# Splitting the involution's DMA transfers by partitions

## The chip, the cores and the metric

The kernel runs on one core of a Trainium2 chip. The metric is the device time of one execution in microseconds; where there are several executions, their median counts. A core has five engines with instruction streams of their own: TensorE (PE in the profile; PEld is its weight loads), VectorE (DVE), ScalarE (ACT), GpSimd (POOL) and SyncE (SP, which here only issues DMAs). Sixteen DMA engines move the data.

## The reference, cut to what matters

The input x is float32 of 8 x 256 x 56 x 56. Layer 0 adds an involution of the normalised x to x; layer 1 adds a residual block of two ternary 3x3 convolutions with batch norm. Only layer 0 is touched by the change:

```python
x = x + _L0_conv_ref(_gn(x), w_reduce, b_reduce, w_span, b_span)     # involution, 7x7, 16 groups
x = x + _L1_conv_ref(_gn(x), w1, w2, g1, b1, g2, b2)                 # two 3x3 convolutions
...
ker = einsum('bchw,oc->bohw', x, w_reduce) + b_reduce                # 256 -> 64 channels
ker = einsum('bchw,oc->bohw', ker, w_span) + b_span                  # 64 -> 16 groups x 49 taps
out = (ker.reshape(B, G, 1, 49, H, W) * patches(xp)).sum(axis=3)     # each pixel has its own 7x7 kernel
```

## The kernel before, in words

The involution (layer 0) comes first, at about 56 to 1108 us of the profile after some 56 us of loads and preparation. The two convolutions and a last pass follow; they read what the involution has stored to HBM (`x1_d`).

The involution goes image by image (8), and in each image through 4 "quarters" of 64 channels, 32 quarters in all. In a quarter the two halves of the image lie on the two halves of the 128 partitions, and 10 rows of tiles (`ty`, each 3 x 8 pixels by 7) are done one after the other. For each row a tile `q` of neighbourhoods is wanted: 126 positions (9 rows by 14 columns around a tile) on the partitions, 7 x 128 values each, read from `x_nb`, which the host lays out. `load_q` issues one DMA of 128 rows (3584 B each) for it; the two rows past 126 belong to the next row or are padding, and nothing reads them. Five buffers (`NQB`) hold q tiles: the tile for row r + 5 is issued by SyncE (`prefetch`) once row r's matmuls have released its buffer. GpSimd then corrects the rims of the tile (`fill_rim`, L752), three rows ahead of its use; for rows 8 and 9 of a quarter ScalarE fills the lower end (`fill_end`, L765), two rows ahead.

TensorE does two things by turns: `apply_row` (pa, L854: 56 small matmuls of q with the kernel matrix `a`) for the present row, and `generate` (pg, L823) for the matrix of the next quarter, whose PSUM results ScalarE (L827) and VectorE (L831) copy into `a` with the bias. ScalarE (L867), VectorE (L868) and GpSimd (L871) bring a row's result out of PSUM and add it onto the image x in SBUF. `reduce` (pk, L711) and the parameters of the next image's normalisation are done in the third quarter (c = 2), from statistics (L143) that VectorE takes of the next image in rows 4 to 19 of the present one.

The order is written out by hand: for each row, in this order, a store of the last quarter's result (`store_x1`, in rows 2 and 3 of a quarter, 64 partitions of 6272 B), or a load of the next image (`load_x`, in rows 0, 1, 4, 5, 7, 8, 14 and 15 of an image, 128 partitions of 3136 B); then `apply_row`, `prefetch`, statistics, `pick_out`, the rims, the steps of `generate`, and one step of the weights' quantisation (loads of 128 x 576 B, L289, and stores of 768 x 192 B, L318). `pin` keeps this order on each engine. All of these DMAs are issued by SyncE, in order. Each takes one of eight completion semaphores by turns and waits until the DMA that had it before, eight issues back, has landed.

Of the kernel before, what the change touches and what calls it, by code (L numbers as in the profile page):

```python
# [17 lines left out]
P = 128  # L18
B, C, H, W = 8, 256, 56, 56
# [9 lines left out]
CH = P // 2  # L29
NCQ = C // CH  # L30
# [3 lines left out]
NHW = HH * W  # L34

PY, PX = 3, 8
TY, TX = 10, W // PX
# [3 lines left out]
QY, QX = PY + K - 1, PX + K - 1  # L41
NQ = QY * QX
# [5 lines left out]
HQ = TY * PY + K - 1  # L48
# [7 lines left out]
NQB = 5  # L56
PLEAD = 2
RIM_AT = 1

NCB = 4  # L60
NC = NHW // NCB
# [22 lines left out]
def involution_tri_block_kernel(  # L84
# [3 lines left out]
    nc = tc.nc  # L88
# [6 lines left out]
    def scratch(name):  # L95
        return [[dram.tile([P, HW], F32, tag=f"{name}_{b}_{t}", name=f"{name}_{b}_{t}")
                 for t in range(CT)] for b in range(B)]

    x1_d, y1_d, y2_d = scratch("x1d"), scratch("y1d"), scratch("y2d")
# [473 lines left out]
    with ExitStack() as ph1:  # L573
# [22 lines left out]
        work = ph1.enter_context(tc.tile_pool(name="work", bufs=2))  # L596
        apool1 = ph1.enter_context(tc.tile_pool(name="apool1", bufs=1))

        def load_x(b, c, j):

            if j == 0:
                xs[b, c] = xpool.tile([P, NHW], F32, tag="x", name=f"x_{b}_{c}")
            part = slice(j * NHW // 2, (j + 1) * NHW // 2)
            nc.sync.dma_start(xs[b, c][:, part], x[b, c, :, part])

        def gn1_stats(b, c, j):

# [56 lines left out]
        prm, xs = {}, {}  # L664
        for c in range(NCQ):
            for j in range(2):
                load_x(0, c, j)
# [28 lines left out]
        for j in range(2):  # L696
            o = j * nf // 2
# [28 lines left out]
        def load_q(b, c, ty):  # L726

            q = qpool.tile([P, TX, P], F32, tag="q", name=f"q_{b}_{c}_{ty}")
            nc.sync.dma_start(q.rearrange("p k c -> p (k c)"),
                              x_nb[b, c, (HQ - QY - PY * ty) * QX:(HQ - QY - PY * ty) * QX + P, :])  # L730
            return q

        def rim_of(b, c):

            sides = work.tile([P, 2, P], F32, tag="sides", name=f"sides_{b}_{c}")
            tops = work.tile([P, 3, CH], F32, tag="tops", name=f"tops_{b}_{c}")
            rim = prm[b][3][:, c]
            for dst, k0, k1, f1 in ((sides, 0, 2, P), (tops, 2, 5, CH)):
                shape = [NQ, k1 - k0, f1]
                nc.gpsimd.tensor_tensor(dst[:NQ], rims_sb[:NQ, k0:k1].unsqueeze(2).to_broadcast(shape),  # L740
                                        rim[:NQ, :f1].unsqueeze(1).to_broadcast(shape), ALU.mult)
            low = work.tile([P, CH], F32, tag="low", name=f"low_{b}_{c}")
            nc.gpsimd.tensor_copy(low[:NQ], rim[:NQ, CH:])
            around[b, c] = sides, tops, low
# [132 lines left out]
        def prefetch():  # L877
            if queue:
                k = queue.pop(0)
                loads[k] = load_q(*k)  # L880
                bare.append(k)

        def surround(keep=PLEAD):
            for k in filled:
                fill_end(*k)
            filled.clear()
            while len(bare) > keep or bare and not queue:
                filled.append(bare.pop(0))
                fill_rim(*filled[-1])

        def store_x1(b, c, h):
            nc.sync.dma_start(
                x1_d[b][c // 2][c % 2 * CH:(c % 2 + 1) * CH, h * NHW:(h + 1) * NHW],
                xs[b, c][h * CH:(h + 1) * CH])

        gst = {}

# [91 lines left out]
        for m, (b, c) in enumerate(quarters):  # L989
# [6 lines left out]
            for ty in range(TY):  # L996
                r = c * TY + ty

                if last is not None and ty in (2, 3):
                    store_x1(*last, ty - 2)  # L1000
                elif more and r in X_AT:
                    load_x(b + 1, X_AT.index(r) // 2, X_AT.index(r) % 2)
                row = apply_row(b, c, a, ty)
                prefetch()

                if r == PARAMS_AT:
                    norm = params(b + 1) if more else gn2_params(0, b)
                next(norm, None)

                if ty == 1 and last is not None:  # L1010
                    gn2_stats(*last, TY)
                elif ty >= 2:
                    gn2_stats(b, c, ty - 1)
                if more and 4 <= r < 20:
                    gn1_stats(b + 1, (r - 4) // NCB, (r - 4) % NCB)
                pick_out(b, c, ty, *row)
                surround()
                if ty == RIM_AT and m + 1 < len(quarters):
                    rim_of(*quarters[m + 1])
                next(norm, None)  # L1020
                for _ in range(PER_ROW[ty]):
                    next(gen, None)
                if m * TY + ty >= QUANT_AT:
                    next(quant, None)
                pin()
# [6 lines left out]
        for h in range(2):  # L1032
            store_x1(*last, h)
# [46 lines left out]
    with ExitStack() as ph4:  # L1080
# [10 lines left out]
        for j in range(B * CT):  # L1091
            b, t = j // CT, j % CT
            y1f, y2f, x1f = (home(name, j) for name in ("y1", "y2", "x1"))
            n = {B * CT - 2: 2, B * CT - 1: 4}.get(j, 1)
# [95 lines left out]
```

## Time and profile before

| what | value |
|---|---|
| median of 3 runs (lowest, highest) | 2209.84 us (2204.62, 2218.38) |
| the profiled execution: time, span | 2220.68 us, 2218.9 us |
| its mean granted TensorE clock | 0.902 |
| TensorE busy over the span | 1765.9 us (80%), 30192 matmuls |
| VectorE, ScalarE, GpSimd busy | 1726.8, 1425.1, 589.8 us |
| q tiles: DMAs, size, median landing | 320, 448 KB, 4.3 us |
| images: DMAs, size, median landing | 64, 392 KB, 5.2 us |
| results: DMAs, size, median landing | 64, 392 KB, 5.5 us |
| one quarter, mean of c = 0, 1, 2, 3 | 30.2, 29.6, 43.1, 27.9 us |

A page of the profile shows one execution. "Busy" counts instructions, not waits. In the list of waits a line such as "ACT q L765 <- POOL q L752: 12.3, 21, 2.1" says that ScalarE was idle before line 765 until GpSimd's line 752 had written q: 12.3 us in total, 21 times, 2.1 us at the longest. "Issue" as the releaser means that the engine was waiting for nothing that the profile names. In the windows each engine has its busy time in the stretch and its count of instructions; behind them stand the granted TensorE clock, the mean busy share of the sixteen DMA engines, and GB/s. A DMA's landing is counted from its issue. The quarters' lengths are from the first pa matmul of one quarter to that of the next.

### The profile page before, as it was taken

The page shows a single profiled execution, that of the slowest core. Times are in us where ns is not written, and L with a number is a line of the kernel's source. Part 1 is how long each engine was busy: PE and PEld are TensorE (multiplying, and loading weights), DVE is VectorE, ACT ScalarE, POOL GpSimd, SP SyncE. Part 2 cuts the span into 40 slices and gives each one's busy share as a digit, 9 for nine tenths or more (in the row PEclk, how much of TensorE's full clock was granted, in tenths as well). Part 3 has the DMA queues.
Part 4 walks back from the last instruction along what each step waited for, and adds up shares of the span by engine and source line. Part 5 has one row for each costly group of instructions (what it writes and reads, how often), then busy time and mean ns, then how long its engine had stood idle before and what let it go on. Part 6 is the DMA issues. An engine that isn't in the chain of part 4 may idle for free.

```text
span 2218.9 us, 71607 instructions
## 1 busy us (share of the span) xinstructions
PE 1765.9 (80%) x30192; PEld 1622.0 (73%) x30192; DVE 1726.8 (78%) x3257; ACT 1425.1 (64%) x3505; POOL 589.8 (27%) x965
## 2 busy tenths in 40 slices
PE   4888898888889888888699999997999999970000
PEld 3676776777667676677599999997999999970000
DVE  5667869686685867756599999998999999984444
ACT  3767677676767767677457666665566666663334
POOL 1546555464654645555500000000000000000000
PEclk9999899899989999899799999999999999995555
DMA  5558768585765757657643333336233333369999
GB/s 179 177 167 250 206 194 250 156 258 180 245 201 166 256 156 242 188 167 207 215 186 119 119 119 118 119 122 212 106 119 119 118 119 124 135 252 414 429 429 396
DMA packets 156252, 440.11 MB, mean 198 GB/s; under 512 B 63774, under 2 KB 74012, under 8 KB 148508
## 3 DMA queue, kind: packets, MB, share of 16 engines
q1 hardware_dynamic: 150336, 405.50, 53.8%
q10 hardware_dynamic: 5596, 30.03, 3.3%
q8 instruction: 239, 3.92, 0.8%
q14 instruction: 81, 0.66, 0.1%
HBM read 323.28 MB, written 112.20 MB: 196 GB/s over the span
## 4 chain that ended last, share of the span: by engine, by line
PE 71%; DMA 10%; DVE 8%; issue 6%; ACT 4%; POOL 0%; SPq 0%; ACTq 0%; DVEq 0%; POOLq 0%
PE c L516 39%; PE pg L823 16%; PE pa L854 10%; PE pk L711 4%; ACT a L827 3%; DMA x1f<-x1d 2%; PE ks L787 2%; DMA y1f<-y1d 2%; DMA out_y<-x1f 2%; DMA y2f<-y2d 2%; DVE a L831 1%; DVE x1f L1103 1%; PE rim L646 1%; DVE st L143 1%; DVE inv L868 1%
## 5 line engine op out<-in xcount | busy, mean ns | idle before, releaser
L516 PE MATMUL c<-pl,wq 128*128 128x392 f32 x4608 | 856.8, 348 | 14.1 <-ACT pl L386 14.1
L516 PEld LDWEIGHTS c<-pl,wq 128*128 128x128 f32 x4608 | 854.8, 189 | 15.8 <-ACT pl L386 14.5
L827 ACT ACTIVATE a<-pg,bt 126x126 f32<-126x126 f32 (+1 forms) x2048 | 528.8, 457 | 113.7 <-PE pg L823 112.0
L823 PE MATMUL pg<-kr,wl 64*126 64x140 f32 (+1 forms) x6144 | 470.1, 297 | 60.7 <-issue 27.8
L823 PEld LDWEIGHTS pg<-kr,wl 64*126 64x126 f32 x6144 | 409.1, 200 | 88.6 <-issue 29.7
L854 PE MATMUL pa<-a,q 126*32 126x48 f32 x17920 | 292.6, 215 | 104.6 <-issue 86.2
L854 PEld LDWEIGHTS pa<-a,q 126*32 126x32 f32 x17920 | 240.8, 117 | 180.0 <-issue 110.0
L831 DVE TENSOR_TENSOR a<-pg,bt 126x504 f32<-126x504 f32 (+4 forms) x640 | 281.3, 481 | 53.7 <-PE pg L823 52.3
L868 DVE SCALAR_TENSOR_TENSOR inv<-pa,gn1s,inv 128x168 f32<-128x168 f32 x320 | 118.3, 370 | 236.2 <-ACT inv L867 235.4
L871 POOL TENSOR_TENSOR x<-x,inv 128x168 f32<-128x168 f32 x320 | 166.6, 521 | 472.5 <-DVE inv L868 386.1
L386 ACT CAST pl<-r 128x812 fp32r<-128x812 f32 x192 | 162.6, 868 | 144.3 <-DVE r L381 124.8
L366 POOL MEMSET xp<- 128x116 f32 x32 | 6.3, 196 | 824.9 <-DVE a L381 824.9
L752 POOL TENSOR_TENSOR q<-q,sides 126x256 f32<-126x256 f32 (+1 forms) x320 | 224.2, 701 | 2.9 <-DMA q<-in_x_nb 2.9
L387 DVE TENSOR_TENSOR pl<-r,pl 128x812 fp32r<-128x812 f32 x192 | 186.8, 999 | 26.5 <-ACT pl L386 25.4
L451 ACT ACTIVATE dummy<-y,nc 128x1568 f32<-128x1568 f32 (+1 forms) x128 | 200.2, 1564 | 4.8 <-DVE y L536 3.5
L867 ACT ACTIVATE inv<-pa,gn1s 128x168 f32<-128x168 f32 x320 | 134.4, 420 | 99.6 <-PE pa L854 72.5
L143 DVE BATCH_NORM_STATS2 st<-x 128x6 f32<-128x392 f32 x256 | 137.8, 554 | 12.3 <-DMA x<-in_x 9.7
L801 POOL TENSOR_TENSOR x<-x,add 128x504 f32<-128x504 f32 (+1 forms) x128 | 127.2, 1025 | 13.1 <-ACT add L795 13.1
L1050 ACT ACTIVATE xp<-raw,gn 128x392 f32<-128x392 f32 (+1 forms) x124 | 82.5, 721 | 58.8 <-DVE a L381 58.8
L1070 ACT ACTIVATE xp<-raw,bi_bn,sc_bn 128x392 f32<-128x392 f32 (+1 forms) x124 | 82.4, 721 | 58.8 <-DVE a L381 57.1
L1101 DVE SCALAR_TENSOR_TENSOR y1f<-y2f,sc_bn,y1f 128x3136 f32<-128x3136 f32 (+2 forms) x20 | 56.6, 2831 | 64.9 <-DMA y2f<-y2d 54.6
L1103 DVE TENSOR_TENSOR x1f<-x1f,y1f 128x3136 f32<-128x3136 f32 (+2 forms) x20 | 55.3, 2771 | 50.2 <-DMA out_y<-x1f 24.2
(174 smaller groups left out, 1791.7 us busy)
## 6 DMA issues: line engine op xcount, KB each, us to landing
q<-in_x_nb SPq DMA_DIRECT2D x320, 448.0 KB, 4.3
raw<-x1d SPq DMA_DIRECT2D x32, 812.0 KB, 6.3
raw<-y1d SPq DMA_DIRECT2D x32, 812.0 KB, 6.5
x<-in_x SPq DMA_DIRECT2D x64, 392.0 KB, 5.2
x1d<-x SPq DMA_DIRECT2D x64, 392.0 KB, 5.5
y1d<-y SPq DMA_DIRECT2D x30, 784.0 KB, 3.8
y2d<-y SPq DMA_DIRECT2D x30, 784.0 KB, 3.3
y1f<-y1d SPq DMA_DIRECT2D x14, 1568.0 KB, 14.3
```

The costliest lines, as they stand in the source:

```text
L143: nc.vector.bn_stats(st[:, j, :], xt[:, j * NC:(j + 1) * NC])
L386: nc.scalar.copy(hi, r)
L387: nc.vector.tensor_tensor(lo, r, hi.bitcast(F32), ALU.subtract)
L451: nc.scalar.activation(dst, v, f, bias=shift[:, to:to + 1], accum_out=stats[:, to, j, n:n + 1])
L516: nc.tensor.matmul(ps[:, to, :NM], wq[k][:, t, dx, to * P:(to + 1) * P], part[:, t, :, dx:dx + W], start=(c == 0), stop=(c == last))
L752: nc.gpsimd.tensor_tensor(v, v, z, ALU.add)
L823: nc.tensor.matmul(dst, wl[rows, c, gp, o:o + NQ], kr[py][rows, px, :], start=True, stop=True)
L827: nc.scalar.activation(dst[:, g + 1, p0 + j], ps[1][:NQ, j * nt + t0:j * nt + t1], AF.Identity, bias=bt[:, c, g + 1, p0 + j:p0 + j + 1])
L831: nc.vector.tensor_tensor(dst[:, g, p0:p0 + n].rearrange("q p t -> q t p"), ps[0][:NQ, t0 * n:t1 * n].rearrange("q (t p) -> q t p", p=n), ...
L854: nc.tensor.matmul(ps[o:o + 32, k * 2 * n:(k + 1) * 2 * n], q[:NQ, k, o:o + 32], av[:, t + k, g * 2 * n:(g + 1) * 2 * n], start=True, stop ...
L868: nc.vector.scalar_tensor_tensor(iv, odd, scale[:, 1:2], iv, ALU.mult, ALU.add)
L871: nc.gpsimd.tensor_tensor(xv, xv, iv.rearrange("p t (y x) -> p y t x", x=PX), ALU.add)
```

## The change

A new helper, `spread`, issues one DMA for each group of partitions, all from SyncE. The q tiles are loaded with 126 partitions instead of 128, in two DMAs whose sizes go by the quarter: 63 + 63 for c = 0, 99 + 27 for c = 1, 108 + 18 for c = 2, 117 + 9 for c = 3. An image's loads become 63 + 63 + 2, a result's stores 63 + 1. The host no longer pads `x_nb`. The instructions of the other engines and their order are the same.

```diff
+SPLITS = ((63, 63), (99, 27), (108, 18), (117, 9))
...
+        def spread(dst, src, cuts):
+
+            p0 = 0
+            for n in cuts:
+                nc.sync.dma_start(dst[p0:p0 + n], src[p0:p0 + n])
+                p0 += n
+
         def load_x(b, c, j):
...
-            nc.sync.dma_start(xs[b, c][:, part], x[b, c, :, part])
+            spread(xs[b, c][:, part], x[b, c, :, part], (63, 63, 2))
...
             q = qpool.tile([P, TX, P], F32, tag="q", name=f"q_{b}_{c}_{ty}")
-            nc.sync.dma_start(q.rearrange("p k c -> p (k c)"),
-                              x_nb[b, c, (HQ - QY - PY * ty) * QX:(HQ - QY - PY * ty) * QX + P, :])
+            o = (HQ - QY - PY * ty) * QX
+            spread(q.rearrange("p k c -> p (k c)"), x_nb[b, c, o:o + NQ, :], SPLITS[(b * NCQ + c) % len(SPLITS)])
             return q
...
         def store_x1(b, c, h):
-            nc.sync.dma_start(
-                x1_d[b][c // 2][c % 2 * CH:(c % 2 + 1) * CH, h * NHW:(h + 1) * NHW],
-                xs[b, c][h * CH:(h + 1) * CH])
+            spread(x1_d[b][c // 2][c % 2 * CH:(c % 2 + 1) * CH, h * NHW:(h + 1) * NHW],
+                   xs[b, c][h * CH:(h + 1) * CH], (63, 1))
...
-    near_rows = np.zeros((B, NCQ, HQ * QX + P - NQ, TX * P), np.float32)
-    near_rows[:, :, :HQ * QX] = near[:, :, ::-1, ::-1].reshape(B, NCQ, HQ * QX, TX * P)
+    near_rows = np.ascontiguousarray(near[:, :, ::-1, ::-1]).reshape(B, NCQ, HQ * QX, TX * P)
```

## The prediction, made before the changed kernel was run

> **What bounds the kernel now.** I read the page's busy table first, then the windows of the involution, then the waits, then the DMA issues, and last the trace's packet records (start, duration, size and queue of each DMA packet; no record names its DMA engine).
>
> The change touches the involution alone, some 56 to 1108 us, and the loads before it. Three stretches (the whole, and one of quarters 0 and 1), with engine busy times, clock, DMA share and GB/s:
>
> ```profile
> 56.00:1108.00 1052.00, 881.26 (x25347) 744.12 (x25343) 746.71 (x2064) 747.06 (x2649) 575.30 (x918) 0.92 0.67 204
> ```
>
> ```profile
> 310.00:390.00 80.00, 66.07 (x2128) 55.02 (x2127) 66.82 (x184) 59.65 (x213) 47.98 (x77) 0.98 0.80 243
> ```
>
> TensorE is busy 84% of the stage, VectorE and ScalarE 71%. The sixteen DMA engines are busy 67%, and 80% where the next image is also loaded. What is late when TensorE idles, over the whole span:
>
> ```profile
> PEld pa L854 <- issue: 110.0, 118, 3.9
> PE pa L854 <- issue: 86.2, 64, 3.7
> ...
> PEld pg L823 <- issue: 29.7, 25, 3.4
> PE pg L823 <- issue: 27.8, 23, 3.2
> ...
> ACT q L765 <- POOL q L752: 12.3, 21, 2.1
> ...
> PEld pa L854 <- POOL q L752: 10.1, 10, 1.6
> ```
>
> "Issue" means that no semaphore was late. (PE and PEld count the same idle time twice.) The reader should see that no DMA of data stands here. What is late is code. Queue 8 carries it:
>
> ```profile
> q8 instruction: 239, 3.92, 0.8%
> ```
>
> 239 packets of 16 KB are 256 instructions each: TensorE's 61,226 rows. In the records TensorE runs at most 449 rows past the 256j-th at which fetch j begins, and then stands until 2.2 to 2.9 us (10 to 90%) after that fetch began. 88 of the 201 fetches of the stage stall it so, 112.7 us in all: 37.5 in quarters 0, 37.8 in quarters 1, 2.3 in quarters 2, 35.1 in quarters 3. What makes a fetch late is data. With the DMA idle for the microsecond before, it begins a median 1.2 us after TensorE passes row 192 of its block and costs 0.02 us of stall; with a share over 0.8 it begins after 2.8 us and costs 0.95 us. And the fetch shares an engine with data: 52 times its record begins 3 or 4 ns after the last record of a data transfer on some engine, and 79 times data resumes 13 to 15 ns before its end; most other offsets nearby have 1 to 4.
>
> [...]
>
> **Which engines a split transfer uses.** One transfer of before shows it, a load of 126 rows next to one of 128:
>
> ```profile
> wl<-in_w_line ACTq DMA_DIRECT2D x1, 644.0 KB, 5.9
> bt<-in_b_tile ACTq DMA_DIRECT2D x1, 189.0 KB
> ```
>
> Its landing is missing, since landings are told only from sixteen signals. In the records two engines carry the neighbouring loads with no row of it between: it ran on 14, the largest divisor of 126 up to 16. I take the same for the rest: 63 rows on 9 engines, 99 on 11, 108 on 12, 117 on 13, and the same first engines each time. One instance carries this. Records with equal starts stand in a fixed order; the one of those two engines that I could follow stands behind its partner in all 6 ties, so I read the order as the engines' number. The fetch's engine stands behind its partners in 61% of 98 ties: about number 9 of 0 to 15, give or take one. So I put 3 in 4 on an engine from the ninth up, which 63-row transfers leave free.
>
> **Part by part.**
> *Issues.* SP gets 320 + 128 + 64 = 512 more DMAs at 0.33 to 0.6 us (medians of its rows), some 200 us. It waits 706.7 us for TensorE to release q tiles (L729), so this is hidden, but for 0.4 us more per tile. Each SP DMA also waits for the one eight issues back, which now covers half as many tiles; with this cover gone, it is part of the late data below. Two fewer rows of q (126, not 128) save nothing.
>
> *Data on the crowded engines.* Record lengths: 140 ns for a q row of 3584 B, 124 for an image row, 239 for a result row. The crowded engines get 14, 12, 11, 10 rows of a q tile by quarter, not 8; 14 image rows, not 8; 7 result rows, not 4; the weight pieces (3.1 us a quarter) stay, since their 128 rows run on all sixteen. Quarter 0 then needs 5 x 1.96 + 5 x 1.68 + 6 x 1.74 + 2 x 1.67 + 3.1 = 35 us (its last five issues are quarter 1's tiles) and lasts 30.2. Quarter 1 needs 26 of 29.6, quarters 2 and 3 need 21 of 43.1 and 23 of 27.9. A queue of about 5 us grows over quarter 0, stays through quarter 1 and is gone in quarter 2. Landings of
>
> ```profile
> q<-in_x_nb SPq DMA_DIRECT2D x320, 448.0 KB, 4.3
> ...
> x<-in_x SPq DMA_DIRECT2D x64, 392.0 KB, 5.2
> x1d<-x SPq DMA_DIRECT2D x64, 392.0 KB, 5.5
> ```
>
> become 9 to 12 us. What there is to spare, from issue to use in the trace: median 8.7 us to POOL's rim fill (L752), 10.1 (least 5.2) to ScalarE's end fill of rows 8 and 9 (L765), 14.0 (least 8.8) to TensorE. The rim fill is late without harm at first. The end fill is not: ScalarE stands on it in order, and the L827 copies that free TensorE's PSUM queue behind it; VectorE's L143 statistics stand on x the same way, some four rows after its load. Late by 2 to 4 us in each of 7 images: 14 us is the low end. If rows run 20% slower on nine engines than alone (their mean record in this stage is 186 ns, not 140), the queue nearly doubles, 10 us an image: 73 is the high end. I take 45, the middle.
>
> [...]
>
> *Before the stage.* 3.2 MB of images over 9 engines at 3136 B per 124 ns: 14 us, not 8, and 24 issues under the eight-back rule, not 8. The chain runs through these loads to 29.0 us ("DMA sums", "DMA q"), so this is on the path: +6 to +14, I take +10.
>
> *Code.* With the fetch on engine 9 or 10 it is alone while quarter 0's tiles are loaded (rows 5 to 9 of quarter 3, 0 to 4 of quarter 0): half of 35.1 and of 37.5, 36 us of stalls, of which 30 go. In the other quarters that engine has 9 rows for 8 but no images and results; I let 12 of the other 76 go. Of these 42, two thirds reach the end: what is late next is ScalarE's L827 and VectorE's L831 (14.3 and 17.7 us of TensorE's idle time already). -28. Ends: 0 if the fetch gains nothing, -85 if three quarters of all 112.7 go.
>
> Sum against the profiled execution, 2220.68 (span 2218.9 and 1.8 around it): +45 + 10 - 28 = +27. That execution lies 10.8 above the median of the runs, 2209.84; so 2237.
>
> **The rivals.**
> 1. *The fetch lives on a crowded engine* (0 to 8). For: nine of sixteen, and the ties are no name. Against: 61%. Each fetch of quarters 0, 1 and 3 then waits 14/8 of today's excess of 2.8 - 1.2 = 1.6 us, +1.2; some 150 fetches (24 of 32 quarters), a little over half exposed: 99 us of stalls, three quarters on the path: +74, +55 from above: 2339.
> 2. *Relief wins* (the other side). One mechanism: the fetch's engine is 11 or above and idle in most quarters, so TensorE no longer stands at row 449. From the point where more than about 70 us of the 112.7 go, it beats a data cost of 14 + 6: -68 + 20 = -48: 2162.
> 3. *The transfers are hidden anyway*: 14 us to TensorE suffices, and only the start and the relief remain: +10 - 28: 2192.
> 4. *It doesn't do what it says*: sixteen engines serve 63 rows. Then 512 issues only: 2210 to 2225. I count it with 3.
>
> **How the numbers follow.** Forecast 0.46 (its own range 2205 to 2275), rival 1 0.24, rival 2 0.18, rivals 3 and 4 0.12. A measurement here can tell about 1%, 22 us, from no change. Slower: 0.27 of the forecast and 0.23 of rival 1, 0.50. Faster: 0.17 and 0.03 of the last group, 0.20. Same: 0.30. The range leaves out a tenth at either end: 2168 to 2365.
>
> **What would show it.** In the profile after: "issue" idle time of TensorE in quarters 0 well under those in quarters 1 (right), or above 150 us in all (rival 1), or under 40 (rival 2). L765 on L752, L143 on x, with over 30 us together, and landings of x above 8 us, show the data cost; the first pk row later than 32.3 us shows the start. If ScalarE and VectorE wait for no tile, the data step is wrong; if landings stay at 4 to 5 us, the engine count is.

## The result, and the profile after

The changed kernel is slower: 2278.43 us (2272.41 to 2282.57) against 2211.69 (2204.62 to 2218.38; four runs, the table above has three), a ratio of 1.030 with a 95% interval of 1.026 to 1.0341. The forecast was 2237; the direction was right, and the loss is two and a half times as large.

The profiled execution took 2278.88 us with a span of 2277.1, 58.2 above the span before. By stretches of the two traces:

| stretch | before, us | after, us | difference |
|---|---|---|---|
| start, to the first pa matmul | 63.5 | 73.2 | +9.7 |
| involution, first pa matmul of the first row of tiles to that of the last | 1040.2 | 1087.1 | +47 |
| convolutions and tail | | | about +2 |

The whole involution in the windows of the changed kernel (stretch and its length, then busy time and count of PE, PEld, DVE, ACT and POOL, granted clock, DMA share, GB/s):

```profile
56.00:1108.00 1052.00, 868.05 (x24181) 725.10 (x24182) 728.22 (x2015) 729.85 (x2583) 551.05 (x876) 0.91 0.61 191
```

In the same 1052 us TensorE did 24,181 matmuls instead of 25,347, and the DMA engines were busy 61% instead of 67%. The 80 us around the third image's first two quarters, as shown before:

```profile
337.00:417.00 80.00, 60.40 (x1831) 50.43 (x1818) 57.29 (x158) 53.02 (x193) 41.65 (x67) 0.91 0.67 215
```

Every engine does less in this stretch, and the DMA engines too (0.67, not 0.80): on average they are idler. That nine of them are full is the forecast's reading; the experiments take it up. These two quarters took 58.1 us before and 70.9 now.

The list of waits after (engine and line, what it waited for: us in total, times, longest):

```profile
PEld pa L862 <- issue: 141.1, 134, 6.5
...
POOL q L760 <- DMA q<-in_x_nb: 109.1, 64, 4.9
PE pa L862 <- issue: 83.6, 63, 6.2
...
DVE piece_w L295 <- DMA piece_w<-in_w: 64.7, 23, 7.7
...
ACT q L773 <- POOL q L760: 56.7, 33, 8.9
...
PEld pa L862 <- POOL q L760: 34.8, 31, 3.3
...
DVE st L144 <- DMA x<-in_x: 23.5, 11, 5.3
```

GpSimd, which had waited 4 us for q, waits 109 us for it; ScalarE's end fill waits 57 us behind GpSimd (12.3 before), VectorE 65 us for weight pieces (none before) and 24 us for images (9.7 before). The same list for SyncE shows where its slack of 706.7 us is:

```profile
SPq L604 <- PE pa L862: 395.8, 159, 36.4
...
SPq L604 <- DMA q<-in_x_nb: 106.9, 148, 1.8
SPq L604 <- DMA x<-in_x: 71.1, 99, 2.0
SPq L604 <- DMA x1d<-x: 45.0, 27, 5.0
```

The last three are the waits on the transfer eight issues back.

"Issue" hides two things here, so I took TensorE's gaps over 60 ns between the first and the last pa matmul from the instruction records. TensorE's program comes in blocks of 256 instructions (in the changed kernel's trace queue 8 has 240 packets of 16 KB for 61,395 instructions), and the forecast found that TensorE stands at instruction 449, counted from the start of a block, until 2.2 to 2.9 us after the next fetch has begun. A gap there is a **fetch stall**; a gap before the first pa instruction of a row of tiles is a **row wait**. Some row waits stand under "issue" too, 36.9 us of them after the change.

| us | before | after |
|---|---|---|
| all gaps in the stage | 165.8 | 198.4 |
| fetch stalls | 112.8 | 82.3 |
| of these in quarters c = 0, 1, 2, 3 | 37.9, 37.9, 2.3, 34.7 | 23.2, 22.9, 7.0, 29.1 |
| row waits | 2.9 | 65.1 |
| TensorE's own instructions in the stage | 875.0 | 889.7 |

So the stage's +47 is +62 of row waits, -30 of fetch stalls, and +15 of TensorE's instructions themselves. That last part fits the granted clock, 0.90 over the stage against 0.92 before. The ks matmuls by shape, before and after (busy us, mean ns):

```profile
L787 PE MATMUL ks<-kr,wsx 64*64 64x504 f32 x384 | 68.3, 660 | 0.0
```

```profile
L795 PE MATMUL ks<-kr,wsx 64*64 64x504 f32 x384 | 78.6, 752 | 0.0
```

Over all ks matmuls the median is 582 ns in both. In the records many take about 1044 (71 of the 384, 26 before): there the granted clock stands at 0.5. The profile's clock changes in steps of 3.41 us; the stage has 51 such windows at half clock before and 61 after.

What a late row looks like. VectorE, and then TensorE's weight load, in the timeline after (start, length, and in brackets the idle time before it and its releaser):

```profile
387.47 0.39 DVE L876 SCALAR_TENSOR_TENSOR inv<-pa,gn1s,inv 128x168 f32<-128x168 f32 x1 [0.90 <-ACT inv L875]
395.56 0.68 DVE L295 TENSOR_SCALAR piece_w<-piece_w,cols 128x144 f32<-128x144 f32 x1 [7.69 <-DMA piece_w<-in_w]
...
399.81 0.56 DVE L144 BATCH_NORM_STATS2 st<-x 128x6 f32<-128x392 f32 x1
...
401.30 0.32 DVE L876 SCALAR_TENSOR_TENSOR inv<-pa,gn1s,inv 128x168 f32<-128x168 f32 x1
```

```profile
401.70 1.19 PEld L862 LDWEIGHTS pa<-a,q 126*32 126x32 f32 x56 [6.32 <-issue]
```

VectorE stands 7.69 us before a weight piece. Behind it in its queue are the statistics and the reading of the last row's PSUM (L876), and TensorE's next row waits 6.32 us for that bank. Going by which engine last raised a semaphore that TensorE stood on, 31 of the 65 us of row waits end with VectorE's L876 and 20 with GpSimd's L760. Of the 65 us, 49 lie in the second half of quarters 0 and the first half of quarters 1.

### The profile page after: what moved, and what is told of

It is laid out like the page before. It is cut to its first block, busy times and chain, and to the rows that moved or that the text cites. A ratio compares the mean times of both kernels' runs of the same rounds, so it can differ in the third digit from the quotient of the medians.

```text
span 2277.1 us, 72688 instructions
## 1 busy us (share of the span) xinstructions
PE 1781.3 (78%) x30192; PEld 1627.0 (71%) x30192; DVE 1730.6 (76%) x3257; ACT 1428.3 (63%) x3505; POOL 592.2 (26%) x965
## 5 line engine op out<-in xcount | busy, mean ns | idle before, releaser
L831 PE MATMUL pg<-kr,wl 64*126 64x140 f32 (+1 forms) x6144 | 470.2, 298 | 49.2 <-ACT a L835 23.3
L831 PEld LDWEIGHTS pg<-kr,wl 64*126 64x126 f32 x6144 | 409.1, 199 | 74.7 <-ACT a L835 28.6
L862 PEld LDWEIGHTS pa<-a,q 126*32 126x32 f32 x17920 | 244.1, 117 | 234.1 <-issue 141.1
L876 DVE SCALAR_TENSOR_TENSOR inv<-pa,gn1s,inv 128x168 f32<-128x168 f32 x320 | 117.7, 368 | 212.9 <-ACT inv L875 211.9
L760 POOL TENSOR_TENSOR q<-q,sides 126x256 f32<-126x256 f32 (+1 forms) x320 | 224.7, 702 | 114.1 <-DMA q<-in_x_nb 87.5
L144 DVE BATCH_NORM_STATS2 st<-x 128x6 f32<-128x392 f32 x256 | 138.1, 554 | 27.0 <-DMA x<-in_x 23.5
L1077 ACT ACTIVATE xp<-raw,bi_bn,sc_bn 128x392 f32<-128x392 f32 (+1 forms) x124 | 82.3, 720 | 58.8 <-DVE a L382 57.1
L1057 ACT ACTIVATE xp<-raw,gn 128x392 f32<-128x392 f32 (+1 forms) x124 | 82.3, 720 | 58.0 <-DVE a L382 58.0
L803 ACT ACTIVATE add<-ks,gn1b,gn 128x504 f32<-128x504 f32 (+1 forms) x128 | 77.1, 677 | 30.6 <-PE ks L795 30.6
```

Source lines behind the costliest of these rows:

```text
L144: nc.vector.bn_stats(st[:, j, :], xt[:, j * NC:(j + 1) * NC])
L760: nc.gpsimd.tensor_tensor(v, v, z, ALU.add)
L831: nc.tensor.matmul(dst, wl[rows, c, gp, o:o + NQ], kr[py][rows, px, :], start=True, stop=True)
L862: nc.tensor.matmul(ps[o:o + 32, k * 2 * n:(k + 1) * 2 * n], q[:NQ, k, o:o + 32], av[:, t + k, g * 2 * n:(g + 1) * 2 * n], start=True, stop ...
```

## The experiments

Fetch stalls and row waits are counted as above, times are medians, and each ratio is to runs of the kernel before on the same chip.

| run | q's transfers; images and results | us | ratio (95%) | fetch | rows |
|---|---|---|---|---|---|
| before | 128; whole | 2211.69 | 1 | 112.8 | 2.9 |
| after | by quarter; split | 2278.43 | 1.030 (1.026, 1.0341) | 82.3 | 65.1 |
| e1 | 64+64; whole | 2242.17 | 1.0148 (1.0112, 1.0184) | 148.3 | 7.5 |
| e2 | by quarter; whole | 2249.54 | 1.0155 (1.0118, 1.0193) | 116.6 | 16.1 |
| e3 | 128; split | 2231.63 | 1.0069 (1.0036, 1.0102) | 108.7 | 18.8 |
| e4 | 63+63; whole | 2246.22 | 1.0151 (1.0122, 1.0181) | 96.6 | 33.6 |
| e5 | two by columns; whole | 2204.02 | 0.9944 (0.9915, 0.9972) | 120.4 | 2.2 |
| e6 | 64 even + 64 odd; whole | 2196.73 | 0.9918 (0.9888, 0.9948) | 111.9 | 6.6 |
| e7 | 126; whole | 2245.76 | 1.0138 (1.0077, 1.02) | 147.7 | 4.0 |
| e8 | by quarter; split but for image 1 | 2268.02 | 1.0223 (1.0159, 1.0287) | 79.8 | 54.4 |
| e9 | none; whole | 2142.31 | 0.9695 (0.9677, 0.9713) | 50.0 | 14.4 |
| e10 | first 63 only; whole | 2162.38 | 0.9771 (0.974, 0.9802) | 53.6 | 11.2 |
| e11 | 64 even only; whole | 2164.32 | 0.9794 (0.9763, 0.9825) | 61.0 | 10.4 |
| e12 | 63 even + 63 odd; whole | 2230.57 | 1.0087 (1.0069, 1.0105) | 97.7 | 30.7 |
| e13 | four of 32; whole | 2380.26 | 1.0733 (1.0683, 1.0784) | 20.3 | 146 |
| e14 | first 63 only; split | 2174.61 | 0.981 (0.9761, 0.9858) | 55.0 | 13.0 |
| e15 | 117+9; whole | 2241.80 | 1.0128 (1.0076, 1.018) | 142.6 | 8.7 |
| e16 | 64 + 32 + 32; whole | 2233.90 | 1.0089 (1.0062, 1.0117) | 72.7 | 33.3 |
| e17 | by quarter; split; pieces later | 2265.26 | 1.0249 (1.0186, 1.0311) | 70.8 | 72.2 |

### The parts of the change

**e1_q_64_64**: as many transfers as the change has for q, but over sixteen engines.

```diff
-SPLITS = ((63, 63), (99, 27), (108, 18), (117, 9))
+SPLITS = ((64, 64),)          # rows o to o + 128; load_x and store_x1 as before
```

> Only the q tiles are split, 64 + 64 rows: twice the DMAs, but every engine still carries 8 rows of each tile, and images and results are whole. Theory 'crowded engines' (the loss comes from 14, 12, 11 or 10 rows on nine engines): no loss, 2200 to 2215, TensorE waits for no q row (under 5 us), fetch stalls about 113 us or less, since the pieces of data that a fetch waits behind are half as long. Rival 'too many DMAs' (the loss comes from SyncE's 512 further issues and from each DMA waiting for the one eight issues back): more than half of the loss, 2235 to 2260, with TensorE standing at the first matmul of a row for 30 us or more.

**e2_q_only**: q as changed, images and results as before.

```diff
-            spread(xs[b, c][:, part], x[b, c, :, part], (63, 63, 2))
+            nc.sync.dma_start(xs[b, c][:, part], x[b, c, :, part])
...
-                   xs[b, c][h * CH:(h + 1) * CH], (63, 1))
+                   xs[b, c][h * CH:(h + 1) * CH], (64,))
```

> The q tiles split as in the change (63+63, 99+27, 108+18, 117+9), images and results whole. Crowded engines: quarter 0 then needs 5 x 1.96 + 5 x 1.68 + 6 x 0.99 + 2 x 0.96 + 3 = 29 us of its 30, so no queue lasts into quarter 1; TensorE's waits at the first matmul of a row fall from 65 us to under 25, the start is as before; 2205 to 2230. Too many DMAs: 320 of the 512 issues are still there, 2240 to 2260.

**e3_x_and_results**: images and results as changed, q whole.

```diff
-SPLITS = ((63, 63), (99, 27), (108, 18), (117, 9))
+SPLITS = ((128,),)            # rows o to o + 128
```

> Images 63+63+2 and results 63+1, q tiles in one DMA of 128 rows. Crowded engines: quarter 0 needs 10 x 1.12 + 6 x 1.74 + 2 x 1.67 + 3 = 28 us of its 30, no lasting queue; the start is 10 us later as in the change; the fetch's engine (9 or 10) carries q and weights only, so fetch stalls fall from 113 to some 85 us: 2200 to 2220. Too many DMAs: 192 further issues, 2225 to 2240 with the start.

**e4_q_63_63**: q on nine engines in all quarters; the rest as in e2.

```diff
-SPLITS = ((63, 63), (99, 27), (108, 18), (117, 9))
+SPLITS = ((63, 63),)
```

> All q tiles 63+63, images and results whole. If the fetch's engine is number 9 or above, it carries no q row at all now: fetch stalls fall from 113 us to under 40. Crowded engines: quarters 0 and 1 need 31 and 27 us of 30, so a small queue and up to 20 us of late rows: 2150 to 2190, faster than both kernels. If the fetch's engine is one of the nine, or if the number of DMAs is what costs: fetch stalls over 113 us or late rows over 50 us, 2240 to 2300.

No theory of these expectations holds in whole. The times of e1, e2 and e3 lie in the ranges of too many DMAs, but the row waits of e1 (7.5 us, not 30 or more) and of e2 (16, under 25) are near what crowded engines would give. Fetch stalls rose in e1 and fell far less than expected in e3 (109 us, not 85) and e4 (97, not under 40), and e4 fits neither side. e5 and e6 below settle the number of transfers.

q alone costs 1.5%, images and results alone 0.7%, together 3.0%: more than the sum. The surplus is in the row waits: 13 and 16 us above those of before in e2 and e3, 62 in the change. So each part alone seems to leave the nine engines room, and both together don't; e14 below tests this.

The engine counts hold. In e4 the records show nine q pieces at once for 280 us of the 920 looked at (80 to 1000 us) and ten, from records that touch, for 8.5 us; before the change the count goes to sixteen. Both halves lie on the same nine engines.

e1 puzzled me. It has hardly more late rows than before, yet loses as much as e4, by fetch stalls (148 us). I first read it as the price of the number of transfers. But its pieces are slower: the median 3,584-byte record is 194 ns, and 140 before and in e4.

**e8_first_image_whole**: the changed kernel, with the first image's loads over 128 partitions.

```diff
-            spread(xs[b, c][:, part], x[b, c, :, part], (63, 63, 2))
+            spread(xs[b, c][:, part], x[b, c, :, part], (63, 63, 2) if b else (P,))
```

> The changed kernel with the first image's sixteen loads whole over 128 partitions; the second image, q and the results as changed. If the start's loss is the first image alone, the first apply matmul comes back from 73.2 to 63.5 us and the time is 2268 (2263 to 2273); the involution stage stays at 1087 us. If the stage's loss followed from how the start leaves the queue, it would shorten too, to 2250 or less.

(The first image has eight loads, not sixteen as the expectation says.) The first pa matmul came back to 63.7 us and the time fell by 10.4; the stage stayed (1091 us). The intervals of the two ratios overlap, so the trace shows this better than the time: the first pa matmul comes at 62.4 to 67.0 us in the fifteen traces with a whole first image, at 70.4 to 73.2 in the four with a split one. The start's loss is the first image, and the stage does not hang on it.

### Number of transfers, place, or rows per engine

**e5_q_columns** and **e6_q_even_odd**: two transfers a tile, each over all partitions. (In the expectation of e5 a half row is wrongly given as 7,168 bytes; it is 1,792.)

```diff
+            for w0 in (0, TX * P // 2):                                        # e5
+                nc.sync.dma_start(qf[:, w0:w0 + TX * P // 2], rows[:, w0:w0 + TX * P // 2])
...
+            for r in range(2):                                                 # e6
+                nc.sync.dma_start(qf[r::2], rows[r::2])
```

> q whole over its 128 rows, but by two transfers of half a row each (7,168 bytes a row); images and results whole as before. As many transfers as with q by rows 64+64, the same bytes, sixteen engines, but each transfer reaches all 128 partitions. Theory of the number of transfers: the time is that of 64+64, 2240 (2232 to 2252), fetch stalls near 148 us. Theory of the place: the median 3,584-byte piece took 140 ns before and 194 ns in 64+64, because there all engines wrote into one half of the partitions at a time; a transfer over all partitions gives back 140 ns, fetch stalls of 105 to 125 us and 2213 (2205 to 2222).

> q by two transfers of 64 rows, the even rows and the odd rows; images and results whole as before. The transfers are those of 64+64 in number, rows, pieces and engines, only the 64 partitions are spread over all 128. Theory of the number: 2240 (2232 to 2252), fetch stalls near 148 us, pieces still near 194 ns. Theory of the place: pieces near 140 ns, fetch stalls 105 to 125 us, 2213 (2205 to 2222).

The place it is. e6 has the transfers of e1 in number, rows and bytes; only the 64 partitions are spread over all 128. The pieces are back at 140 ns, the fetch stalls at 112 us, and the 30 us lost against the kernel before are gone. (The rows read from HBM alternate in e6 too; no run separates this from the partitions, but the neighbouring rows of e4 were read in 140 ns apiece.) Into 64 neighbouring partitions the median piece took 1.39 times as long; why, no run shows.

Both came out faster than the kernel before, by 0.6 and 0.8%, below their ranges. The window of e6, and SyncE's wait:

```profile
56.00:1108.00 1052.00, 886.79 (x25474) 750.52 (x25472) 777.13 (x2105) 760.28 (x2670) 576.08 (x919) 0.94 0.70 211
```

```profile
SPq L740 <- PE pa L864: 355.6, 184, 37.1
```

The clock is 0.94 instead of 0.92. There are 6 gaps of 3 us and more instead of 11, 33 half-clock windows instead of 51. Why the long gaps are fewer was not settled. But two transfers a tile are no cost here, as the forecast had it.

**e7_q_126** and **e15_q_117_9**: nine rows on an engine instead of eight, in one transfer and in two.

```diff
-            spread(q.rearrange("p k c -> p (k c)"), x_nb[b, c, o:o + NQ, :], SPLITS[(b * NCQ + c) % len(SPLITS)])
+            nc.sync.dma_start(q[:NQ].rearrange("p k c -> p (k c)"), x_nb[b, c, o:o + NQ, :])   # e7
...
-SPLITS = ((63, 63), (99, 27), (108, 18), (117, 9))
+SPLITS = ((117, 9),)                                                                     # e15
```

> q as one transfer of its 126 rows, nine rows on each of fourteen engines if the largest divisor counts; images and results whole; as many transfers as before. Theory that the fetch lies on one of the first fourteen engines (about the ninth) and that nothing but its queue counts: 9 rows instead of 8 ahead of it, fetch stalls 113 to 127 us, 2212 to 2228. If the fetch lay on the fifteenth or sixteenth engine: fetch stalls under 60 us and 2160 to 2180. If only the number and place of transfers count: 2212 (2205 to 2219).

> q by 117+9 rows in all quarters (nine rows on each of thirteen engines and one row on each of nine); images and results whole. The row of 126 rows on fourteen engines cost 1.4%: nine rows instead of eight ahead of a fetch. If nine rows on the fetch's engine are what counts, the same here: 2240 (2230 to 2255), fetch stalls near 145 us. If it was something of the one long transfer, 2212 (2205 to 2222).

e7 lies above all its ranges; e15, expected after it, came as the ninth row would have it. One row more on the engines of a tile costs 22 to 39 us of fetch stalls against the runs with eight such rows (108.7 to 120.4 us: before, e3, e5, e6), and over 1% of the time. That e15 agrees with e7 although it has twice the transfers speaks for the rows. (e1 shows the same stalls with eight rows an engine, but slower ones.) I had forecast a small gain in the quarters with 99, 108 and 117 rows.

**e13_q_four** and **e16_q_three**: more transfers still, over all partitions.

```diff
+            for r in range(4):                                                 # e13
+                nc.sync.dma_start(qf[r::4], rows[r::4])
...
+            for r, m in ((0, 2), (1, 4), (3, 4)):                              # e16
+                nc.sync.dma_start(qf[r::m], rows[r::m])
```

> q by four transfers of 32 rows, every fourth row, all partitions and sixteen engines; images and results whole. Against even and odd 64+64 (2197, ratio 0.992) only the number of transfers grows, by 640. If the number is a gain, 2185 (2175 to 2192); if it does nothing, 2197 (2190 to 2205); if it costs, as it would if the issues came onto the path, above 2210.

> q by three transfers over all partitions and sixteen engines: the 64 even rows, then the odd rows in two transfers of 32; images and results whole. SyncE's waiting for the apply matmuls was 707 us with one transfer, 356 with two of 64 rows and 74 with four. If SyncE is the bound only when that waiting is gone, some 150 to 220 us are left with three and the time is 2195 (2185 to 2212). If its issues already hold up rows, the time lies between two and four, 2250 to 2300, with over 40 us of waits at a row's first apply matmul.

Here the number does cost. In e13 the waits are

```profile
POOL q L762 <- DMA q<-in_x_nb: 241.4, 125, 4.1
...
ACT q L775 <- POOL q L762: 151.2, 48, 7.1
...
PEld pa L864 <- POOL q L762: 96.6, 61, 4.7
```

```profile
SPq L740 <- PE pa L864: 73.5, 24, 32.1
```

SyncE has hardly any slack left, so q is issued late. An issue of 64 or 32 rows over sixteen engines holds SyncE a median 588 to 592 ns in e6, e13 and e16 (587 in e1), one of 128 rows 328 ns, one of 63 rows on nine engines 278 ns in e4. Four of the first are 2.4 us a tile, one of the second 0.33: times 320, 650 us more, about the 633 us by which SyncE's wait falls. With three (e16) 143.7 us of waiting are left, and still rows are late for 33 us, outside both of the expected ranges: slack averaged over a stage is not slack at each tile. And where rows are late, fetch stalls shrink (20 us in e13). A part of them goes under the row waits, since a fetch goes on while TensorE waits for something else (a fetch record overlaps 16 of the 42 row waits of the changed kernel): without the row waits, by an estimate from the records that lets TensorE go on 2.2 to 2.7 us after each fetch begins, 26 to 37 us more would show in e13, and 6 in the kernel before. The larger part is fetches that begin sooner, a median 1.34 us after TensorE passes instruction 192 of the block, against 2.42 before.

### What a fetch waits for

**e9_no_q**, **e10_q_first_63**, **e11_q_even_64**: after the first five tiles, no q rows, 63 on nine engines, or 64 on sixteen. The missing rows keep old values.

```diff
+            if k < NQB:
+                nc.sync.dma_start(qf, src)
+            else:                                      # e9: no else
+                nc.sync.dma_start(qf[:63], src[:63])   # e10; e11: [::2]
```

> q is loaded only for the first five rows of blocks, whole; every later row of blocks works on what stands in those five tiles, so the results are not the reference's: 315 of 320 q loads are left out. Images and results whole as before. Both theories of the fetch (it waits behind data on its own engine; it waits for the traffic as a whole) expect stalls of 15 to 40 us instead of 113 and a time of 2140 (2115 to 2165). If fetch stalls do not come from the q transfers at all they stay near 113 us and the time near 2213.

> As the run without q, but each later row of blocks loads the first 63 of its 128 q rows, seven on each of nine engines; the other rows stay as they are, which leaves out half of the q bytes. Theory of the own engine (the fetch's engine is not among the nine, as the records of the changed kernel suggest): fetch stalls as without q, 15 to 45 us, 2140 (2115 to 2170). Theory of the traffic as a whole: 45 to 75 us, the same as with 64 rows on all engines, 2165 (2145 to 2185).

> As the run without q, but each later row of blocks loads its 64 even q rows, four on each of sixteen engines, over all partitions: the bytes of the run with the first 63 rows, with the fetch's engine among the carriers. Theory of the own engine: 50 to 80 us of fetch stalls, well above the first 63, 2170 (2150 to 2190). Theory of the traffic as a whole: like the first 63, 45 to 75 us, 2165 (2145 to 2185).

q's transfers make 63 of the 112.8 us of fetch stalls; 50 remain without any, ten more than expected. The DMA share falls to 0.29 and 0.51 (these windows run some 80 us past the end of the shortened stage; in the stage alone it is 0.28 and 0.53):

```profile
56.00:1108.00 1052.00, 930.58 (x25736) 792.64 (x25733) 820.20 (x2169) 786.09 (x2708) 577.14 (x921) 0.94 0.29 77
```

```profile
56.00:1108.00 1052.00, 921.28 (x25702) 786.22 (x25699) 812.53 (x2160) 777.26 (x2700) 577.00 (x921) 0.94 0.51 145
```

The first window is e9's, the second e10's. Between equal bytes with and without the fetch's engine (e11, e10) lie 7 us of fetch stalls, and the intervals of the two times overlap. e10's 54 us are more than the own engine allowed in figures (45), but only 4 above the run without q, and "as without q" was that theory's point. e11 fits both. There is one trace of each, so no spread is known against which to hold 7 us, and these runs do not separate the theories.

**e12_q_63_63_even_odd**: e4 with its rows spread over all partitions.

```diff
+            for r in range(2):
+                nc.sync.dma_start(qf[r:NQ:2], rows[r::2])      # 63 rows each
```

> q by two transfers of 63 rows, the even and the odd rows of its 126; seven rows on each of nine engines, images and results whole, everything as in the run with q 63+63 but for the partitions that a transfer reaches. Theory of the place: its loss against even and odd 64+64 (2197) was the half of the partitions, so 2200 (2190 to 2215), fetch stalls 70 to 95 us. Theory of the nine engines: they carry fourteen rows each instead of eight and late rows cost what they cost in 63+63 (26 us): 2240 (2232 to 2250).

0.6% better than e4, no more; fetch stalls and row waits stay. Here the nine engines are what costs, not the place, though the time is just under their range. And 97 us of fetch stalls stay in both, though q seems mostly off the fetch's engine: in e6 129 q pieces begin 13 to 15 ns before the end of a fetch of the stage, in e4 42, where the offsets around would give 28 and 24.

### Which late data

**e14_half_q_in_changed**: the changed kernel, but each later q tile loads its first 63 rows alone.

```diff
-            spread(q.rearrange("p k c -> p (k c)"), x_nb[b, c, o:o + NQ, :], SPLITS[(b * NCQ + c) % len(SPLITS)])
+            spread(qf, src, (P,) if k < NQB else (63,))
```

> The changed kernel, images and results in 63-row transfers, but of each q after the first five only the first 63 rows are loaded, on nine engines; the other rows stay as they are, so half of the q bytes and the results' rightness are left out. If the late rows come from the load on the nine engines, the waits at a row's first apply matmul fall from 65 us to under 20, fetch stalls to 45 to 60, and the time is 2185 (2165 to 2205), start included. If the late rows came from images and results alone, the waits stay over 40 us and the time over 2205.

Row waits fall from 65 to 13 us. The load on the nine engines is the cause. Fetch stalls are 55.0, and 53.6 in e10, which differs only in that images and results run on sixteen engines there: taking them off the fetch's engine brought nothing.

**e17_pieces_later**: the changed kernel; the weight pieces get one more step to land.

```diff
-            for n, f in ((0, fetch), (2, ternary), (3, planes_of), (5, store)):
+            for n, f in ((0, fetch), (3, ternary), (4, planes_of), (6, store)):
```

> The changed kernel; only VectorE takes up each weight piece of the quantisation one step later (its ternary part three steps after the load instead of two, the planes four, the store six). In the trace of the changed kernel 31 of the 65 us of waits at a row's first apply matmul end with VectorE's reading of the row before, which stands behind weight pieces that landed late (VectorE waits 64.7 us for them). If that is the cause, VectorE's waits for the pieces fall under 20 us, the rows' waits to about 35, and the time to 2250 (2240 to 2262). If TensorE would have waited for late q rows behind them anyway, the time stays at 2278 (2268 to 2285).

13 us, between the two expectations; the intervals of the two ratios (1.0249 and 1.030) overlap. VectorE's waits for the pieces fell to 19.4 us and its share of the row waits from 31 to 7 us, but GpSimd's rose from 20 to 59:

```profile
POOL q L760 <- DMA q<-in_x_nb: 151.9, 75, 4.4
...
PEld pa L862 <- POOL q L760: 79.0, 47, 3.5
```

The late weight piece was the last of two; behind it the q row was late as well. Row waits did not fall (72 us). In the traces the gain lies in fetch stalls (-11.5 us) and in pg's waits for ScalarE and VectorE (L831, 31.7 to 19.5 us).

## Why the prediction was wrong in size

Point by point, by its own steps.

- **Engines of a split transfer: right in number.** Nine for 63 rows and the same nine each time, fourteen for 126 (e7: at most 14 q pieces at once, but for 2.4 us of touching records), thirteen for 117 (quarters 3 of the changed kernel: at most 13, but for 7.5 us). Which one carries the fetch stays open. Rival 4 falls with it: the change does what it says. Rival 3 falls with the 62 us of row waits: the transfers were not hidden.
- **Before the stage, +10: right.** 9.7 us by the trace, 10.4 by the times of e8; the first pk row moved from 32.2 to 42.0 us.
- **Data on the crowded engines, +45 within 14 to 73: mis-sized, the larger of the two gaps in the sum.** The row waits grew by 62 us. The mechanism is the one named, shown by e14 (13 us with half of q). The place is right too: 49 of the 65 us fall where the queue was to stand, late in quarters 0 and early in quarters 1. Two signs came: L773 on GpSimd 56.7 and L144 on images 23.5 us. What it had wrong: "the weight pieces stay, since their 128 rows run on all sixteen". Nine of these sixteen are the crowded ones, and VectorE, which stands on the pieces in order, waited 64.7 us for them. With later pieces (e17) the row waits stayed, behind late q rows, so the step was short in the q rows as well. Landings of 9 to 12 us can't be read: a split transfer has no landing in the profile.
- **A term that was missing: +15 for TensorE itself.** The step priced a stall at its length. A long one is followed by half clock (numbers in the last section), and the sum has no term for that; the stage has 14 gaps of 3 us and more after the change, 11 before, and ten more half-clock windows, worth at most 17 us.
- **Code, -28: the size came out (-30) by luck; the reason failed.** It said that the fetch's engine is relieved while quarter 0's tiles load, in rows 5 to 9 of quarters 3 and 0 to 4 of quarters 0, and booked 30 us of stalls there. The stalls in these rows went from 27.3 to 26.2 us. They fell in the next ones, the last half of quarters 0, the first of quarters 1 and the first of quarters 3: from 63.5 to 32.5 us. Freeing that engine of images and results gave nothing (e14 beside e10), nine rows on it in all quarters cost 22 to 39 us (e7, e15), where the forecast let 12 go in the quarters that have nine. In e13, with the latest rows and q on all sixteen engines as before, the stalls fell most. By the same estimate as there, 19 to 24 us of stalls lie under row waits in the changed kernel and 6 before, so about half of the -30 is stall time that goes under another wait. The other half is fetches that begin sooner (a median 1.85 us after instruction 192, against 2.42). Why they do, and what a fetch still waits for in e4, is open.
- **Issues, 0: right at two transfers a tile** (e5, e6). It doesn't carry over to more: at four, SyncE is the bound (e13).
- **The sum.** +10 + 62 - 30 + 15 + 2 is 59, against 58 by the spans; the forecast's +27 lacks 17 of late rows and 15 of clock. The medians differ by 66.7, since the execution profiled before lay 9 us above its median.
- **A sign that misled.** "Above 150 us of issue" was to mean rival 1, a fetch on a crowded engine. The lists after give 141.1 and, for pg, 17.2; but 36.9 us of row waits stand under that name, and the fetch stalls are 82. Rival 1 and rival 2 both rested on the fetch's engine; neither the rise nor the large fall of fetch stalls that they needed came.

## What to carry to other kernels

Before a transfer is narrowed to fewer engines, add up all that these engines then carry, the untouched transfers on them too, and follow each late landing through the queue of the engine that waits: the one that stands first hides the next. Don't book less of one stall as a gain of its own while another wait grows in the same place: look whether it fell where the reason says it should, and how much of it only lies under the new wait. If a transfer must be cut, cut it so that each part reaches all partitions (2197 us in e6, 2242 in e1), and count the issues: two per tile were free here (ratios of 0.994 and 0.992 in e5 and e6), three were not (1.009 in e16).

## What the runs showed of the hardware

- **Half of the partitions.** Sixteen engines writing 64 neighbouring partitions: 194 ns for the median 3,584-byte piece; 64 alternate ones, 140 ns (e1, e6). Nine engines into 63 neighbouring ones: 140 ns as well (e4). e6 also alternates the rows that it reads.
- **Issue time.** A SyncE issue held its queue 328 ns for 128 whole rows, 278 for 63 rows on nine engines, 587 for 64 rows on sixteen, 713 for 63 alternate rows on nine (medians of before, e4, e1, e12). Where one 64-row issue a tile stands alone, it is 474 (e11).
- **Half clock.** In the nineteen traces of this case together, 177 of 183 TensorE gaps of 3 us and more in the stage had a stretch of half clock in them or within 3.5 us, 347 of 563 gaps of 1.5 to 3 us, 214 of 900 of 0.7 to 1.5 us. Stretches of the same lengths at random places of the stage have half clock in 38, 31 and 28%: gaps of 1.5 to 3 us had one twice as often as chance, and the shortest show nothing. What told the drops apart was the idle share of a window: in the 3.41 us ahead of a drop TensorE was idle for a median 64%, and over half of the time in 443 of 536 drops; that was so ahead of 16 of 4,830 windows at full clock.
- **The step at the ninth row.** With q on thirteen engines or more, 4, 8 and 9 q rows on an engine per tile came with fetch stalls of 61, 109 to 120, and 143 to 148 us (e11; before, e3, e5 and e6; e15 and e7); in e1, with eight slower rows, 148. One row is 140 ns a tile; why the ninth costs so much was not found. With q on nine engines the stalls were 54 us at 7 rows (e10) and 97 at 14 (e4, e12).
- **A fetch's start.** The median fetch record lasts 0.97 to 1.21 us in all nineteen traces. What varies is its start: a median 1.3 us (e13, e14) to 2.8 us (e15) after TensorE passes instruction 192 of the block.
